# Four graph layers in one kernel: the end of the first output chunk of the second pass comes four products later

## The chip, the cores and the metric

The kernel runs on one core of a Trainium2 chip. The metric is the device time of one execution in microseconds (us). The time before is 1056.23 us, the median of three runs (1054.62 to 1058.79). The profile is one more execution, with a time of 1041.55 us.

## The reference

A graph of N = 2708 nodes has a sparse-looking but densely stored weight matrix `adj` (N x N, f32) and 128 features a node (`x`). Four layers follow one another, each as `x = layernorm(x + layer(x, adj))`. What matters here is layer 0 and the start of layer 1:

```python
# layer 0
z = leaky_relu(lap_mul(A, x) @ W1 + b1, 0.1)
S = exp(-sqrt(max(|z_i - z_j|^2, 0) + 1e-10) / 2), kept for the 4 nearest rows j of each i, else 0
out = lap_mul(S + A, x) @ W2 + b2          # lap_mul(A, x) = d * (A @ (d * x)), d = rowsum(A)^-1/2
# layer 1
XW = X @ W;  s_col = XW @ a[:128];  s_row = XW @ a[128:]
den = exp(leaky_relu(s_row[:, None] + s_col[None, :], 0.01))
num = A @ den;  att = den / num;  H = A @ (att @ XW)
# layer 2: normalized adj @ x, a linear map;  layer 3: relu of a linear map of [x, adj @ x]
```

The product `(S + A) @ (d * x)` of layer 0 is the second pass over `adj`: a dense part, `A` times the scaled rows, and a sparse part, four gathered rows for each node, weighted by their similarity. From the result layer 1 needs the rank of every node by `s_col`, which the kernel finds by comparing every pair.

## The kernel before

Nodes are cut into T = 22 tiles of 128 (the last has 20 rows), and the columns of the transposed output into six chunks: four of 512, one of 384 and one of 276. Chunk 0 holds tiles 0 to 3, chunk 1 tiles 4 to 7, and so on.

The second pass is `by_panels` (line 189). For each chunk c it multiplies 21 row tiles (and, for three chunks together, the short last tile) into one PSUM tile `acc`: the `product` at line 204 has the scaled rows `y2` (name `y` in the profile) as weights and a stretch of `adjT` as moving data. One product is two MATMUL entries in the trace. Row tiles 16 to 21 of `adjT` stay in SBUF (`res`), the others come from memory in panels of four row tiles (1 MB, line 178, issued on SP) into four slots of `ring`. A slot is filled again when the four products that read it are done.

Between the products everything else of the pass is put by hand. TensorE, VectorE (DVE) and ScalarE (ACT) run in exactly the order in which the program names their instructions (`manual_schedule`, line 1064). `Due` (line 31) is a list of work with due counts: `due.tick()` runs after each product, counts up by one, and issues all work that is due. I call this number the count. GpSimd (POOL) and SP are not under the manual order.

The work with due counts:

- `sum_near(t)` (line 765), at the counts 20 + (24 t) // 5, so 20, 24, 29, 34, 39, 44, 48, 53, 58 for tiles 0 to 8. On POOL three indirect DMAs (line 759) each gather 128 rows of 512 bytes from memory into one of nine `got` buffers; on DVE one TENSOR_SCALAR (line 768) and three SCALAR_TENSOR_TENSOR (line 772) add them up, each of the three behind its own gather.
- `end_pass2(c, acc)` (line 1014), called when chunk c has its last product. It puts the end of the chunk on a count n, and all that follows from it on n plus a fixed number:
  - n: `add_near` (line 774), which multiplies the chunk's `near_sum` tiles with the identity into `acc` on TensorE (line 779, two MATMUL entries a tile), and the copy of `acc` to `hT` on ACT (line 1021);
  - n + 2: `norm0`, the product with W2 (line 809), the residual on DVE (line 814), and the layer norm (lines 272 to 277);
  - n + 9: `turn`, the transposes of the normalized rows on TensorE (line 827) and their copy on ACT (line 830);
  - n + 11: `find_c`, one product (line 883), its copy (line 884) and four reductions on DVE (line 888);
  - n + 13 and later, every second count: `compare` on DVE (lines 924 and 934), `times_w` (line 896 on TensorE, 897 on ACT), `rank_rows` on ACT (line 942), `rank_columns` on TensorE (line 947), and `keep_xw`, a DMA from POOL (line 902).

The count n is the largest of three: the next count, the count of the chunk's last `sum_near` plus 3, and the last chunk's n plus 16. For the six chunks this gives 37, 56, 75, 95, 111 and 132. For chunk 0, whose products end at count 21, it is the second term: tile 3 is due at 34, so n = 37.

The order of row tiles in chunk 0 is 0 to 11, 16 to 19, 12 to 15, 20. In chunk 1 the four products of the panel with row tiles 12 to 15 are those of the counts 37 to 40.

Of the kernel before, what the change touches and what calls it, by code (L numbers as in the profile page):

```python
# [30 lines left out]
class Due:  # L31
# [5 lines left out]
    def at(self, n, f, *args):  # L37
        self.work.append((n, len(self.work), f, args))
        self.work.sort(key=lambda w: w[:2])
# [13 lines left out]
def kernel(  # L53
# [47 lines left out]
    chunk_tiles = [range(a // P, (a + w + P - 1) // P) for a, w in zip(starts, cw)]  # L101
# [262 lines left out]
    with tc.tile_pool(name="knn", bufs=1) as knn:  # L364
# [68 lines left out]
        due = Due()  # L433
# [340 lines left out]
    def add_near(c, acc):  # L774
        ts = chunk_tiles[c]
        for t in ts:
            p = pw[t]
            o = t * P - starts[c]
            nc.tensor.matmul(
                acc[:, o : o + p], lhsT=near_sum[:p, t, :], rhs=ident[:p, :p], start=False, stop=(t == ts[-1])  # L780
            )
# [214 lines left out]
    due = Due()  # L996
    at = due.at
    near_at = [20 + (24 * t) // 5 for t in range(T)]
# [11 lines left out]
    ended = [-16]  # L1010
# [1 line left out]
    behind_turn = []  # L1012

    def end_pass2(c, acc):
        n = max(due.n + 1, near_at[chunk_tiles[c][-1]] + 3, ended[-1] + 16)
        ended.append(n)
        ts = chunk_tiles[c]

        def finish():
            add_near(c, acc)  # L1020
            nc.scalar.copy(hT[:, cols[c]], acc[:, : cw[c]])

        at(n, finish)
        if c < C - 1:
            at(n + 2, norm0, ts)
            at(n + 9, turn, c)
            at(n + 11, find_c, c)
            if c == C - 2:
                for t in behind_turn:
                    at(n + 11, rank_rows, t)  # L1030
            for k, t in enumerate(ts):
                at(n + 13 + 2 * k, compare, t)
                at(n + 14 + 2 * k, times_w, c, t)
                if k == len(ts) - 1:
                    at(n + 14 + 2 * k, keep_xw, c)
                if c == C - 2 and k == len(ts) - 1:
                    behind_last.append(t)
                elif c == C - 3 and k == len(ts) - 1:
                    behind_turn.append(t)
                else:  # L1040
                    at(n + 16 + 2 * k, rank_rows, t)
                if t:
                    at(n + (20 if c < C - 2 else 18) + 2 * k, rank_columns, t)
        else:
            for t in behind_last:
                at(n + 1, rank_rows, t)
            at(n + 2, norm0, ts, True)
            at(n + 2, turn, c, True)
            at(n + 2, exp_table)
            at(n + 2, find_r)  # L1050
            at(n + 3, last_stats)
            at(n + 3, last_of, 1, cc)
            at(n + 3, turn_c, c)
            at(n + 3, compare_known, ts[0])
            at(n + 5, last_of, 0, rr)
            at(n + 5, negate_r)
            for k, t in enumerate(ts[:-1]):
                at(n + 4 + k, compare, t)
                at(n + 4 + k, rank_rows, t)
                at(n + 5 + k, rank_columns, t)  # L1060
            at(n + 3 + len(ts), compare_few)
            at(n + 4 + len(ts), exp_r)

    with tc.manual_schedule(engines={nc.tensor.engine, nc.vector.engine, nc.scalar.engine}):
        by_panels(
            rows_of(y2), end_pass2, due.tick, ready, [*range(S - 4), *range(S, T - 2), *range(S - 4, S), T - 2]
        )
        due.flush()
# [814 lines left out]
```

## Time and profile before

| what | value |
|---|---|
| median of three runs | 1056.23 us |
| the profiled execution: time, span | 1041.55 us, 1039.7 us |
| TensorE busy over the span | 973.5 us (94%) |
| DVE, ACT, POOL busy | 639.0, 332.2, 261.0 us |
| mean granted TensorE clock | 0.983 |
| second pass in the span | about 285 to 418 us |
| dense products in it (line 204), each of two entries | about 0.86 us each at 512 columns |

The profile's page gives shares over the whole span; all times inside the second pass below are microseconds from the span's start. In a timeline an entry has its start, its length and, in brackets, how long the engine stood idle before it and what ended that. "PE" is TensorE. In a table by windows each engine's busy time in that stretch is followed by the number of instructions in brackets, and the columns at the end are the granted TensorE clock (1.00 is full), the busy share of the DMA engines, and GB/s.

### The profile page before, as it was taken

The numbers are of one execution on the slowest core, as the hardware profiler recorded it, in microseconds if no ns is written. First come the engines' busy times: TensorE is split into PE (matmuls) and PEld (weight loads), VectorE is DVE, ScalarE is ACT, GpSimd is POOL, SyncE is SP. The second block draws the span as 40 slices with busy tenths as digits, with TensorE's granted clock in tenths as the row PEclk, the third lists the DMA queues.
The fourth block names the chain that finished last, engine by engine and source line by source line (L and its number), as shares of the span: only waits on it lengthen the run. The fifth ranks groups of instructions, "written<-read, shape, count | busy, mean of one in ns | idle before, by whom it ended". The sixth has DMA issues, their size and how long they took to land.

```text
span 1039.7 us, 11663 instructions
## 1 busy us (share of the span) xinstructions
PE 973.5 (94%) x3773; PEld 476.7 (46%) x3773; DVE 639.0 (61%) x1364; ACT 332.2 (32%) x609; POOL 261.0 (25%) x339
## 2 busy tenths in 40 slices
PE   0789999999998999797999999999999999999996
PEld 0346554444444557563333333334445544564444
DVE  5886438999955678865899999992212021222222
ACT  0000126555501236505777777661101100020000
POOL 4000000000557664027565444420111100000000
PEclk9999999999998999799999999999999999999999
DMA  9999240000175757696465455556565856475652
GB/s 328 373 365 314 91 152 1 0 1 1 43 240 183 236 171 239 236 409 204 144 163 158 131 144 160 143 178 238 165 229 151 310 181 224 137 273 173 212 179 68
DMA packets 101985, 191.00 MB, mean 184 GB/s; under 512 B 14006, under 2 KB 43326, under 8 KB 101914
## 3 DMA queue, kind: packets, MB, share of 16 engines
q1 hardware_dynamic: 83880, 152.34, 43.5%
q0 software_dynamic: 17728, 37.62, 12.6%
q8 instruction: 32, 0.52, 0.2%
q14 instruction: 39, 0.32, 0.1%
q10 hardware_dynamic: 306, 0.20, 0.1%
HBM read 214.80 MB, written 4.16 MB: 211 GB/s over the span
## 4 chain that ended last, share of the span: by engine, by line
PE 50%; DVE 1%; ACT 1%; issue 0%; DMA 0%; POOL 0%; POOLq 0%; DVEq 0%
PE acc L204 28%; PE hacc L1571 10%; PE num L1689 10%; PE mis L285 1%; PE mis L1818 0%; DVE inv L1560 0%; DMA ring<-carry 0%; ACT gb L234 0%; DVE err L1556 0%; PE mis L1784 0%; DVE inv L1563 0%; PE mis L1814 0%; POOL rstd L253 0%; PE mis L1772 0%; ACT m_rows L160 0%
## 5 line engine op out<-in xcount | busy, mean ns | idle before, releaser
L1689 PE MATMUL num<-ring,lw 128*64 128x512 f32 (+1 forms) x528 | 112.1, 557 | 5.4 <-DMA ring<-carry 2.9
L1123 POOL DMA_INDIRECT ring<-in_adjT,slot_i x88 | 92.9, 1056 | 96.6 <-PE num L1689 77.5
L1571 PE MATMUL hacc<-inv,xws 128*128 128x512 f32 (+1 forms) x264 | 111.7, 559 | 0.3 <-DVE inv L1563 0.3
L714 PE MATMUL acc<-zT,z 128*128 128x512 f32 (+2 forms) x252 | 102.2, 552 | 0.0
L1546 ACT ACTIVATE inv<-num,plain 128x1024 f32<-128x1024 f32 x88 | 80.6, 916 | 59.0 <-PE num L1689 43.1
L253 POOL TENSOR_TENSOR rstd<-rstd,minus_half 128x4 f32<-128x4 f32 (+1 forms) x18 | 17.3, 959 | 311.8 <-DVE rstd L252 311.8
L234 ACT COPY gb<-acc 128x512 f32<-128x512 f32 (+2 forms) x18 | 9.6, 534 | 249.4 <-PE acc L204 249.4
L715 ACT COPY key<-acc 128x512 f32<-128x512 f32 (+2 forms) x126 | 67.1, 534 | 55.1 <-PE acc L714 27.7
L204 PE MATMUL acc<-ring,y 128*128 128x512 f32 (+2 forms) x192 | 82.1, 557 | 0.5 <-issue 0.5
L1571 PEld LDWEIGHTS hacc<-inv,xws 128*128 128x128 f32 x264 | 46.6, 189 | 77.8 <-issue 33.5
L1556 DVE TENSOR_TENSOR err<-inv,num 128x1024 f32<-128x1024 f32 x88 | 74.7, 853 | 10.1 <-ACT inv L1549 8.9
L759 POOL DMA_INDIRECT got<-y_rows,where x66 | 71.4, 1081 | 34.6 <-DVE near_sum L772 13.5
L1563 DVE SCALAR_TENSOR_TENSOR inv<-gb,g_inv,inv 128x1024 f32<-128x1024 f32 x88 | 77.0, 913 | 0.1
L204 PE MATMUL acc<-ring,xs 128*128 128x512 f32 (+2 forms) x192 | 76.7, 542 | 0.0
L204 PE MATMUL acc<-ring,carry 128*128 128x512 f32 (+2 forms) x192 | 74.5, 542 | 0.0
L204 PE MATMUL acc<-ring,m_rows 128*128 128x512 f32 (+2 forms) x192 | 74.3, 542 | 0.0
L1560 DVE SCALAR_TENSOR_TENSOR inv<-err,inv 128x1024 f32<-128x1024 f32 x88 | 72.4, 861 | 0.1
L714 PEld LDWEIGHTS acc<-zT,z 128*128 128x128 f32 x252 | 45.8, 190 | 50.4 <-issue 44.9
L1549 ACT ACTIVATE inv<-inv 128x1024 f32<-128x1024 f32 x88 | 67.6, 768 | 2.8
L1689 PEld LDWEIGHTS num<-ring,lw 128*64 128x64 f32 x528 | 36.1, 137 | 62.9 <-issue 48.1
L584 POOL TENSOR_TENSOR slot_e<-near,sim 128x44 f32<-128x44 f32 (+2 forms) x3 | 0.7, 237 | 254.5 <-DVE near L581 254.4
L718 DVE MAX8 near<-key 128x8 f32<-128x2708 f32 x21 | 62.3, 2965 | 2.6 <-ACT key L715 2.6
(379 smaller groups left out, 1355.7 us busy)
## 6 DMA issues: line engine op xcount, KB each, us to landing
ring<-in_adjT SPq DMA_DIRECT2D x74, 1024.0 KB
ring<-in_adjT SPq DMA_DIRECT2D x20, 677.0 KB
ring<-in_adjT SPq DMA_DIRECT2D x17, 768.0 KB
part<-in_adjT SPq DMA_DIRECT2D x12, 1024.0 KB
ring<-in_adjT SPq DMA_DIRECT2D x17, 552.0 KB
more<-in_adjT SPq DMA_DIRECT2D x10, 677.0 KB
res<-in_adjT SPq DMA_DIRECT2D x4, 1280.0 KB
part<-in_adjT SPq DMA_DIRECT2D x3, 768.0 KB
```

The source lines that it names most:

```text
L204: nc.tensor.matmul(accs[c][: lhsT.shape[-1], :w], lhsT=lhsT, rhs=src, start=start, stop=stop)
L714: nc.tensor.matmul(pks[c][:p, : cw[c]], lhsT=z2[:, :p], rhs=zT[:, cs], start=False, stop=True)
L715: nc.scalar.copy(key[:p, cs], pks[c][:p, : cw[c]])
L759: nc.gpsimd.indirect_dma_start(out=got[:p, :], out_offset=None, in_=y2_rows[:, :], in_offset=bass.IndirectOffsetOnAxis(ap=where[:p, t, k : ...
L1123: nc.gpsimd.indirect_dma_start(out=rows[i][:KC, n, :], out_offset=None, in_=adj_half[:, :], in_offset=bass.IndirectOffsetOnAxis(ap=slot_i[ ...
L1546: nc.scalar.activation(inv, num[:, :w], AF.Ln, scale=plain[:, 0:1], bias=plain[:, 1:2])
L1549: nc.scalar.activation(inv, inv, AF.Exp, scale=-1.0)
L1556: nc.vector.tensor_mul(err, inv, num[:, :w])
L1560: nc.vector.scalar_tensor_tensor(inv, err, 2.0, inv, op0=ALU.subtract, op1=ALU.mult)
L1563: nc.vector.scalar_tensor_tensor(inv, gb[:, col : col + w], g_inv[:, q : q + 1], inv, op0=ALU.max, op1=ALU.mult)
L1571: nc.tensor.matmul(haccs[:, o:e], lhsT=xws[:, q, :], rhs=inv[:, o:e], start=(q == 0), stop=(q == NQ - 1))
L1689: nc.tensor.matmul(num[n * (BJ + 2) : (n + 1) * (BJ + 2), o:e], lhsT=lw[:, 2 * q + n, :], rhs=rows[i][:, n, c0 + o : c0 + e], start=True, ...
```

## The change

One number in `end_pass2` is replaced: chunk 0 now ends at least 7 counts after its last `sum_near`, the other chunks still at least 3.

```diff
     def end_pass2(c, acc):
-        n = max(due.n + 1, near_at[chunk_tiles[c][-1]] + 3, ended[-1] + 16)
+        n = max(due.n + 1, near_at[chunk_tiles[c][-1]] + (3 if c else 7), ended[-1] + 16)
         ended.append(n)
```

The counts n of the six chunks become 41, 57, 75, 95, 111 and 132. Chunk 0 moves by four; chunk 1 moves by one, because it has to stay 16 behind chunk 0; the others stay. No instruction is added or removed. The order of the instructions on POOL and SP stays as it was. On TensorE, DVE and ACT the work of chunks 0 and 1 changes places with its neighbours: on DVE `sum_near` of tile 7 now stands ahead of the first `compare` of chunk 0, the `compare` of tile 3 behind the layer norm of chunk 1, and `sum_near` of tile 10 ahead of the reductions of `find_c` for chunk 1; on ACT and TensorE the end of chunk 1 comes earlier among the row sums and the `times_w` of chunk 0.

## The prediction

> **What bounds the kernel now.** Over the span TensorE is busy 94%, so only its losses in the second pass count. I read first the second pass by windows: before the end of chunk 0, around it, the long middle, the end.
>
> ```profile
> core 0: us, PE busy (x) PEld busy (x) DVE busy (x) ACT busy (x) POOL busy (x), PEclk, DMA share, GB/s
> 285.00:314.45 29.45, 29.45 (x73) 12.65 (x72) 16.05 (x44) 2.43 (x11) 16.93 (x31) 1.00 0.73 243
> 314.45:325.00 10.55, 6.38 (x21) 4.11 (x20) 3.06 (x8) 1.87 (x2) 8.11 (x9) 0.68 0.52 173
> 325.00:415.00 90.00, 88.84 (x468) 52.99 (x468) 67.52 (x253) 33.71 (x72) 54.33 (x51) 1.00 0.65 205
> ```
>
> TensorE is full up to 314.45 and almost full after 325.00. Between, it is busy 6.38 of 10.55 us, and at a clock of 0.68. So the second view is TensorE's timeline there:
>
> ```profile
> 314.45 0.83 PE L779 MATMUL acc<-ident,near_sum 128*128 128x128 f32 x6
> 319.46 0.80 PE L779 MATMUL acc<-ident,near_sum 128*128 128x128 f32 x2 [4.17 <-DVE near_sum L772]
> 320.05 3.62 PE L204 MATMUL acc<-ring,y 128*128 128x512 f32 x4
> 323.46 1.80 PE L809 MATMUL mis<-w,hT 128*128 128x128 f32 x8
> 325.10 1.02 PE L204 MATMUL acc<-ring,y 128*128 128x512 f32 x2
> 325.96 4.46 PE L204 MATMUL acc<-res,y 128*128 128x512 f32 x10
> ```
>
> At 314.45 chunk 0 ends: three tiles of near rows go through (x6), the fourth stands 4.17 us for DVE. After it four entries of the dense product take 3.62 us; later ten take 4.46. The clock by windows, cut where it changes, says why (same columns):
>
> ```profile
> 314.77:318.18 3.41, 0.52 (x5) 0.32 (x3) 0.70 (x2) 0.00 (x0) 2.74 (x3) 1.00 0.93 309
> 318.18:321.60 3.42, 2.14 (x4) 1.27 (x5) 0.91 (x3) 1.29 (x2) 2.51 (x4) 0.50 0.39 126
> 321.60:325.00 3.40, 3.40 (x11) 2.21 (x10) 1.44 (x4) 0.58 (x1) 2.79 (x3) 0.50 0.20 59
> 325.00:328.40 3.40, 3.40 (x10) 1.62 (x10) 2.76 (x13) 0.14 (x1) 2.49 (x4) 1.00 0.40 90
> ```
>
> The nearly idle window is followed by 6.8 us at half clock. Last, DVE's timeline: what the fourth tile waits for.
>
> ```profile
> 315.79 0.74 DVE L772 SCALAR_TENSOR_TENSOR near_sum<-got,sim,near_sum 128x128 f32<-128x128 f32 x2 [1.96 <-DMA got<-y_rows,where]
> 319.06 0.35 DVE L772 SCALAR_TENSOR_TENSOR near_sum<-got,sim,near_sum 128x128 f32<-128x128 f32 x1 [2.53 <-DMA got<-y_rows,where]
> 319.32 0.43 DVE L768 TENSOR_SCALAR near_sum<-y,own_sim 128x128 f32<-128x128 f32 x1
> 321.39 1.13 DVE L772 SCALAR_TENSOR_TENSOR near_sum<-got,sim,near_sum 128x128 f32<-128x128 f32 x3 [1.63 <-DMA got<-y_rows,where]
> 322.43 0.68 DVE L1002 TENSOR_TENSOR xs<-xs,b 128x512 f32<-128x512 f32 x1
> 325.30 1.13 DVE L814 SCALAR_TENSOR_TENSOR xs<-mis,d2inv,xs 128x128 f32<-128x128 f32 x4 [2.19 <-PE mis L809]
> ```
>
> Its third gather has landed only at 319.06, and DVE is free before. The gathers start at 298.93 and POOL issues one every 1.30 us; none of the first twelve waits for a product. So tile 3 is ready at 319.41 whatever TensorE does: the end of chunk 0 comes too early for the gathers. This wait is the only one of TensorE in the pass over 1.3 us.
>
> [...] the gathers issued between 312 and 318, beside panel loads, take a median of 5.4 us to land, those between 322 and 330 take 2.5. [...]
>
> **The change part by part.** No instruction is added or removed, and POOL's and SP's orders stay.
>
> Part 1, the loss now. From 314.45 to 325.96 (11.51 us) TensorE does the near rows of four tiles, three dense products and eight entries of the W2 product. At full clock, from undisturbed places of this trace: 0.89 us (341.66 to 342.55), 3 x 0.858 (ten entries at 325.96 take 4.29 to the next start), 0.89 (344.49 to 345.38), together 4.35. The loss is 11.51 - 4.35 = 7.16 us: 4.3 of standing still (tile 3 due at 314.45 + 6 x 0.111 = 315.12, started at 319.46) and 2.8 of half clock.
>
> Part 2, what remains of it. Four products go ahead: the end of chunk 0 starts at 314.45 + 4 x 0.858 = 317.88, tile 3 is due at 318.55 and comes at 319.46 as before. Remaining wait 0.91 us. Does the clock hold? The trace bounds it: with 2.65 of 3.41 us busy (406.93:410.34) it stayed at 1.00, with 1.96 of 3.41 (417.17:420.58) it fell. A window with 0.9 us of idling is 2.5 busy, near the first. I take no throttle: half clock 0 (bound: one window, 1.7 us).
>
> Part 3, the DMA that moves along. In chunk 1 the last of the four products reading a ring slot is that of count 40. Before, it was over at 326.1, behind the stall, and SP issued the panel load at 326.15. Now it comes before the end of chunk 0, at about 317.0, and the 1 MB load goes out nine us earlier, right behind the one of 313.79. Tile 3's gathers are issued before that (the last at 313.53), so I leave 319.41. But the last gather of tile 4 is issued at 317.44, after the load. By the semaphore events of the trace these panel loads land 5.1 to 7.3 us after issue, so this one at 322.1 to 324.3, and with it that gather, instead of at about 321.7.
>
> Part 4, who waits for that. On DVE `sum_near` of tile 4 stands ahead of the bias (0.68 us) and the layer norm of chunk 0. If nothing slips, DVE is through the bias at 323.11; the W2 product, now at full clock, is at 319.68 + 2 x 0.858 = 321.4 to 322.3. So the norm starts at 323.1 instead of 325.3. It takes 4.5 us (325.30 to 329.83): done at 327.6. The transposes need it, seven products after W2: 322.3 + 7 x 0.858 = 328.3. Slack 0.7. With the gather landing at 322.1 to 324.3, the norm starts at about 323.3 to 326.1 (0.35 for the last addition, 0.68 the bias, some overlap of 0.1 each) and ends at 327.8 to 330.6: TensorE waits 0 to 2.3 us there. I take a landing of 323.1, so a wait of 0.7; both ends go into the range.
>
> Part 5, the rest of the moved chain keeps its cover. Copy to `hT` on ACT: 0.58 us under two products (1.72), as before. `find_c` to `compare` on DVE: same counts apart. `sum_near` of tile 7 now stands ahead of the compares: gathers issued up to 329.5, landed by 334 to 335, added by 336; chunk 1 ends at count 57, about 337 with part 4's wait, its fourth tile 0.7 later. If that cover were gone it would cost what the landing is late. `compare` of tile 3 and `times_w` of tile 3 move behind chunk 1's norm in DVE's and ACT's queues; the row DMA to memory that needs them stands in POOL's queue at 346.27 and needs them by about 344, so it isn't held. Chunk 1's one product more is not work, only order: 0.
>
> Part 6, does the lead survive? DVE stands 4.1, 4.2, 1.9 and 4.5 us for TensorE between 341 and 377 and POOL stands 3.9, 2.8, 1.3 and 3.1 us for freed buffers between 346 and 379, so both can follow 5 to 6 us earlier. From 377 to 415 DVE has under 1 us of gaps, but that stretch begins behind a TensorE product and moves with it. From chunk 2's norm on every order is the old one. After the pass the line loads start when TensorE has freed the ring, so they move too. I take all of it as kept.
>
> The sum: 7.16 - 0.91 - 0.7 = 5.5 us. Against the profiled execution: 1041.55 - 5.5 = 1036.0. The median of the runs is 14.7 us above that execution; I carry the same difference over: 1056.23 - 5.5 = 1050.7, or 0.52% less.
>
> **The rivals.**
>
> Rival 1, the clock falls again: tile 3 or the transposes wait more than about 1.4 us inside one window (1.96 of 3.41 busy was enough). For it: part 3's load lands late, 324.3, giving a wait of 2.3. Against: usual landings are nearer 5.2. Price: 1.6 more waiting and 1.7 for one window at half clock: gain 5.5 - 3.3 = 2.2; 1.5 to 4.5 with smaller slips. Time 1054.0.
>
> Rival 2, the lead is given back at the end of the pass: DVE is busy 8.9 of 10 us and ACT 9.7 of 10 in its last 20 us, and TensorE already waits there for masks (1.2 and 1.1 us). If they don't start earlier, gain 0 to 2: 1055.2. Against: part 6.
>
> Rival 3, slower: the held-back gather of tile 4 makes a larger stall at the transposes than the one removed. Place: DVE's queue, gather, bias, norm, then TensorE at count 50. Price: [...] the loss is 0.91 + s + 2.8 against 7.16. From s = 3.5, a landing at about 325.9, it is even; slower by 0.5% (5.3 us) needs s = 8.7, a landing at 331, over 13 us after issue, where the trace has at most some 6.5. Time then 1062.
>
> Rival 4, in the timed runs the old stall is longer than in the profiled one (they are longer altogether, and the profile doesn't say where): four products can absorb up to 3.43 us of wait, the half clock could be longer: gain 7 to 9, time 1048.
>
> That the change doesn't do what it says is excluded: the counts come out of the code as 41 and 57.
>
> **How the numbers follow.** Forecast (gain 4.8 to 6.3) 0.62; rival 1 0.20; rival 2 0.08; rival 3 0.04; rival 4 0.06. About 0.5% (5.3 us) is what a measurement of this kernel can tell from no change. It cuts through my forecast: of 0.62 I put 0.44 above it; with rival 4 faster 0.50. Within 0.5%: 0.18 of the forecast and rivals 1 and 2, 0.46. Slower: 0.04. The range: the forecast alone 1049.9 to 1051.4, with the scatter of a median of runs (the three lie 1.6 below and 2.6 above) 1048 to 1054; to rival 4 below and rival 1 above, it becomes 1046.5 to 1055.
>
> **What would show it.** Right: line 779's wait falls from 4.17 to about 0.9 us, the clock stays 1.00 between 314 and 330, a panel load is issued near 317 and not at 326, chunk 1 ends at count 57 at about 337 instead of 341.66. Part 4: a wait of up to 2.3 us at line 827 for DVE's norm. Wrong: a clock of 0.50 in that stretch, tile 3's last addition later than 320, or chunk 5's end less than 4 us earlier than 415.02.

## The result, and the profile after it

| | before | changed |
|---|---|---|
| median of 22 runs each | 1057.16 us | 1057.76 us |
| lowest to highest | 1051.42 to 1061.24 | 1048.95 to 1063.06 |
| ratio, 95% interval | | 1.0015 [0.9997, 1.0033] |
| profiled execution: time, span, clock | 1041.55, 1039.7, 0.983 | 1057.04, 1055.2, 0.976 |

The change makes no difference that can be measured. I had forecast 1050.7 us, and the result lies outside my range.

A sitting is one series of runs, with the kernel before run again in it. The kernel before took 1040.2 to 1042.5 us in two of the seven sittings (this result is one of the seven) and 1056.7 to 1060.6 in the other five; two chips showed both. I call these short and long sittings. The profile shown ahead of the prediction is one of the short kind; the runs beside it, and the profile after, are of the long kind.

The second pass of the changed kernel by windows, cut where the end of chunk 0 begins, where the loss is over, and at the last chunk's near rows (columns as before):

```profile
285.00:317.91 32.91, 32.91 (x82) 14.17 (x80) 18.39 (x50) 2.44 (x11) 20.48 (x35) 1.00 0.70 233
317.91:339.00 21.09, 9.32 (x28) 5.29 (x27) 4.90 (x20) 2.08 (x3) 8.43 (x9) 0.68 0.37 127
339.00:425.98 86.98, 83.74 (x453) 50.13 (x452) 64.36 (x236) 33.35 (x71) 50.06 (x46) 1.00 0.62 197
```

The first window is full, up to 317.91 and no longer to 314.45: the four products have gone ahead. But then TensorE is busy 9.32 of 21.09 us, where before it was 6.38 of 10.55. Its timeline there:

```profile
317.91 1.05 PE L779 MATMUL acc<-ident,near_sum 128*128 128x128 f32 x8
318.80 1.88 PE L204 MATMUL acc<-res,y 128*128 128x512 f32 x4
332.45 2.08 PE L809 MATMUL mis<-w,hT 128*128 128x128 f32 x8 [11.77 <-ACT hT L1021]
334.32 3.62 PE L204 MATMUL acc<-res,y 128*128 128x512 f32 x4
337.74 4.79 PE L204 MATMUL acc<-ring,y 128*128 128x512 f32 x10
```

The wait of the prediction is gone: all eight entries of line 779 go through in one group. In its place the product with W2 (line 809), two products later, waits 11.77 us for ACT's copy of `acc` to `hT`. The clock by windows:

```profile
320.70:324.70 4.00, 0.00 (x0) 0.00 (x0) 0.95 (x2) 0.00 (x0) 3.08 (x4) 1.00 0.24 73
324.70:328.10 3.40, 0.00 (x0) 0.00 (x0) 0.00 (x0) 0.00 (x0) 2.49 (x4) 0.51 0.14 39
328.10:331.50 3.40, 0.00 (x0) 0.00 (x0) 0.00 (x0) 0.00 (x0) 0.68 (x1) 0.50 0.13 39
```

TensorE, DVE and ACT do next to nothing together; only POOL works. The clock is halved from 324.7 for 13.7 us. In the profiles before and after the stretches of half clock last 3.41, 6.83 or 13.65 us, save the last one of each (6.88 and 8.98 us). Why does the copy start so late? ACT's timeline has it at

```profile
331.81 0.59 ACT L1021 COPY hT<-acc 128x512 f32<-128x512 f32 x1 [36.09 <-remote]
```

although the matmuls that it needs were over at 318.96. ACT was free for 36 us, and "remote" means that the profile finds no event on this core that released it. The trace has the missing piece in the times at which TensorE's completions were counted in its semaphore (from here on "count" means this, not the due count of `Due`): those of the matmuls that ended about 317 to 319 were all counted between 330.89 and 331.79, in one burst, up to 13.7 us late. In the profile before, each such count comes within 0.3 us. SP's panel loads, which wait for the same semaphore, are held alike: line 178 issues one at 316.20 and the next only at 330.91. POOL's timeline shows what ends in between:

```profile
326.47 1.00 POOL L759 DMA_INDIRECT got<-y_rows,where  x1 [0.30 <-issue]
327.78 1.00 POOL L759 DMA_INDIRECT got<-y_rows,where  x1 [0.30 <-issue]
339.95 1.00 POOL L759 DMA_INDIRECT got<-y_rows,where  x1 [11.17 <-DVE near_sum L772]
```

From 297.64 on POOL has issued 24 gathers without a break. At 328.78 its nine buffers are all taken, it stops, and 3.0 us later the copy starts. DVE is not late with the near rows but stands, too:

```profile
317.10 0.74 DVE L772 SCALAR_TENSOR_TENSOR near_sum<-got,sim,near_sum 128x128 f32<-128x128 f32 x2
321.68 0.35 DVE L772 SCALAR_TENSOR_TENSOR near_sum<-got,sim,near_sum 128x128 f32<-128x128 f32 x1 [3.84 <-DMA got<-y_rows,where]
321.95 0.68 DVE L1002 TENSOR_TENSOR xs<-xs,b 128x512 f32<-128x512 f32 x1
334.57 1.13 DVE L814 SCALAR_TENSOR_TENSOR xs<-mis,d2inv,xs 128x128 f32<-128x128 f32 x4 [11.93 <-PE mis L809]
```

Tile 3's rows are added by 316.8, tile 4's last at 322.0. So the question is: is the late counting a thing of the changed order, or was it in the timed runs of the kernel before as well?

### The profile page after: what moved, and what is told of

Its sections match the earlier page's. It is cut to its first block, busy times and chain, and to the rows that moved or that the text cites. A ratio compares the mean times of both kernels' runs of the same rounds, so it can differ in the third digit from the quotient of the medians.

```text
span 1055.2 us, 11662 instructions
## 1 busy us (share of the span) xinstructions
PE 980.4 (93%) x3773; PEld 478.9 (45%) x3773; DVE 640.1 (61%) x1364; ACT 332.4 (32%) x609; POOL 261.8 (25%) x339
## 4 chain that ended last, share of the span: by engine, by line
PE 49%; DVE 1%; ACT 1%; issue 0%; DMA 0%; POOL 0%; POOLq 0%; DVEq 0%
PE acc L204 28%; PE hacc L1571 10%; PE num L1689 9%; PE mis L285 1%; PE mis L1818 0%; DVE inv L1560 0%; DMA ring<-carry 0%; ACT gb L234 0%; DVE err L1556 0%; PE mis L1784 0%; DVE inv L1563 0%; PE mis L1814 0%; POOL rstd L253 0%; PE mis L1772 0%; ACT m_rows L160 0%
## 5 line engine op out<-in xcount | busy, mean ns | idle before, releaser
L204 PE MATMUL acc<-ring,y 128*128 128x512 f32 (+2 forms) x192 | 79.6, 548 | 0.5 <-issue 0.5
```

Source lines behind the costliest of these rows:

```text
L204: nc.tensor.matmul(accs[c][: lhsT.shape[-1], :w], lhsT=lhsT, rhs=src, start=start, stop=stop)
```

## The experiments

Where the expectations name theories by letters, A says that late counts come in both kernels and depend on the sitting; B that the changed order brings them about; C that they are held while POOL issues gathers without a break, so that the stall ends when POOL runs out of buffers; D that panel loads or chance hold them. All times after a colon are medians; every ratio is to the kernel before in the same sitting.

### Both kernels again, chunk 0 without gathers, and seven made eleven

e1 is the kernel before unchanged, e2 the changed one. e3 is the kernel before without the gathers and additions of tiles 0 to 3 (their near rows are left out of the sum). e4 takes the change further.

```diff
 # e3
-        for k in range(TOPK - 1):
+        for k in range(TOPK - 1 if t > 3 else 0):
 # e4
-... near_at[chunk_tiles[c][-1]] + 3, ended[-1] + 16)
+... near_at[chunk_tiles[c][-1]] + (3 if c else 11), ended[-1] + 16)
```

> The kernel before, unchanged, with a second profile. Theory A: the late semaphore counts of TensorE (13.7 us late in the profile after, ACT and TensorE idle for 11.8 us) come in ordinary executions of either kernel, and the first profile of before, at 1041.55 us, was an exceptional one: this profile shows a span near 1052 to 1056 with a stall of about 10 us in the second pass that is not the wait for near_sum alone. Theory B: the late counts come with the changed order only: this profile shows a span near 1040, one stall of 4 us at line 779 and no other over 2 us in the second pass. Time ratio 1.00 in both.

> The changed kernel, unchanged, with a second profile. Theory A: in some profiles a stall of about 10 us at the first copy of acc or the W2 product, in others none and then a span of about 1036. Theory B: the stall of 11.8 us at the same instruction again. Time ratio 1.00 in both.

> The kernel before with the gathered rows of tiles 0 to 3 left out (near_sum there is only the node's own row), so that the end of chunk 0 at count 37 waits for no gather. If the wait for near_sum and its half clock are what costs (my prediction's part 1): 7.2 us less than before, ratio 0.993. Theory A: another stall takes its place in most executions and the ratio lies between 0.997 and 1.002. Theory B: 7.2 us less.

> Chunk 0 ends at count 45 (11 after its last near_sum), chunk 1 at 61, chunk 2 at 77. By the prediction's reasons: the wait at line 779 is gone altogether and tile 4's gather has time, 6 to 7 us less than before (ratio 0.994). Theory A: ratio 0.998 to 1.003 as the change of four had, with the stall at whatever waits first for TensorE's count. Theory B: the stall of 12 us at the copy of acc again, ratio about 1.00.

Measured, with the kernel before at 1042.54 us (33 runs), so in a short sitting: e1 1043.16, ratio 1.0008 [0.9993, 1.0022]; e2 1038.26, **0.9951 [0.9930, 0.9972]**; e3 1039.76, 0.9978 [0.9968, 0.9989]; e4 1036.91, 0.9937 [0.9916, 0.9957]. The long stall came in none of the four, so what these expectations say of it stays unanswered here. In time the changed kernel (five runs) gains what the prediction said, e4 (five runs) what its expectation said; e3 misses its 0.993. TensorE's timeline in e2:

```profile
318.20 0.83 PE L779 MATMUL acc<-ident,near_sum 128*128 128x128 f32 x6
320.11 0.49 PE L779 MATMUL acc<-ident,near_sum 128*128 128x128 f32 x2 [1.07 <-DVE near_sum L772]
320.43 1.88 PE L204 MATMUL acc<-res,y 128*128 128x512 f32 x4
322.15 1.05 PE L809 MATMUL mis<-w,hT 128*128 128x128 f32 x8
323.04 1.88 PE L204 MATMUL acc<-res,y 128*128 128x512 f32 x4
324.76 4.45 PE L204 MATMUL acc<-ring,y 128*128 128x512 f32 x10
330.08 1.10 PE L827 MATMUL mis<-ident,xs 128*128 128x128 f32 x4 [0.87 <-DVE xs L277]
```

A wait of 1.07 us for tile 3 where I had 0.91, one of 0.87 at the transposes where I had 0.7, no half clock in this stretch, a panel load at 317.54 where I had about 317. DVE's line for the last near row of tile 4:

```profile
325.40 0.35 DVE L772 SCALAR_TENSOR_TENSOR near_sum<-got,sim,near_sum 128x128 f32<-128x128 f32 x1 [4.36 <-DMA got<-y_rows,where]
```

The pass shows the lead, and how more than half of it is lost: counted from the pass's first product, the end of chunk 1 comes at 54.1 us (e1: 56.8), though it stands one product of 0.86 us later in the changed order, so the lead there is 3.6 us of work; the end of chunk 5 comes at 128.5 (e1: 130.1), a lead of 1.6. These two executions are not typical: e1's is the shortest of its twelve (1039.01 us), e2's the longest of its five (1040.88). So the traces don't show where the whole gain of the medians lies. e3 gains more inside the pass (chunk 5 at 123.9) and less in all: its trace has the clock halved for 13.1 us at the very end, where e1 has 9.4, and once more at 937.9.

### The kernel before in a long sitting

f1 is the kernel before, unchanged, profiled where it is slow.

> The kernel before, unchanged, once more, in the hope of a chip on which it takes 1057 us as in the comparison of the result, not 1042 as in the last runs. Theory A (the late semaphore counts belong to such a chip, whatever the kernel): if the time is near 1057, the profile shows a stall of some 10 us behind a late count in the second pass, fewer semaphore events recorded than in the first profile, and a granted clock near 0.976. Theory B (they belong to the changed order): no such stall, and the 15 us are spread or lie elsewhere. If the time is near 1042 it tells nothing new.

Measured: 1061.08 against 1060.52, ratio 1.0006 [0.9993, 1.0018]. TensorE's timeline of f1:

```profile
313.92 0.83 PE L779 MATMUL acc<-ident,near_sum 128*128 128x128 f32 x6
316.82 0.49 PE L779 MATMUL acc<-ident,near_sum 128*128 128x128 f32 x2 [2.06 <-issue]
317.14 3.29 PE L204 MATMUL acc<-ring,y 128*128 128x512 f32 x4
333.39 2.08 PE L809 MATMUL mis<-w,hT 128*128 128x128 f32 x8 [12.96 <-ACT hT L1021]
```

The same stall, in the same place, in the kernel before: B falls, A stands. The wait for tile 3, from which my whole sum was made, is 2.06 us here and is followed by 12.96 us for the copy. POOL again issues 24 gathers, the last over at 329.70, and the copy starts at 332.75, 3.05 us later. This one execution took 1066.16 us, the most of its twelve and 5.1 above their median. With that taken off, as if all of it lay in the pass, chunk 5 ends 144.2 us after the pass's start (149.3 in the trace) by my estimate, in the changed kernel at 142.0 (its execution 0.7 below its median) and in g1, below, at 140.5 (5.6 below). The two kernels' passes are alike.

### Chunk 0 without gathers, and fewer buffers, in a long sitting

g1 is the changed kernel, g2 is e3's kernel again, with the same near rows left out; g3 and g4 are the kernel before and the changed one with five buffers for gathers in place of nine, so that POOL has to stop earlier.

```diff
-    got_pool = late.enter_context(tc.tile_pool(name="got", bufs=9, side="right"))
+    got_pool = late.enter_context(tc.tile_pool(name="got", bufs=5, side="right"))
```

> The changed kernel again. Two conditions have been seen: before at 1042 us (there the change gave a ratio of 0.995) and before at 1057 to 1061 (there 1.0015). Theory C: in the slow condition TensorE's counts are held back as long as POOL issues gathers without a pause, so the copy of acc to hT comes when POOL has run out of got buffers (about 331 to 333), wherever the end of chunk 0 stands: ratio 0.995 to 1.003, stall of 11 to 13 us in front of the W2 product. Theory D: the held-back count is a matter of the panel loads or of chance, not of POOL. In the fast condition: 0.995 again.

> The kernel before without the gathered rows of tiles 0 to 3 (left out). POOL then has 12 gathers less and runs out of buffers at about 314, before the end of chunk 0. Slow condition, theory C: no stall at the copy of acc, 12 to 20 us less than before (ratio 0.981 to 0.989). Theory D: the stall stays, at most 4 us less. Fast condition: 0.998 as before.

> The kernel before with five got buffers instead of nine: POOL must stop four gathers earlier, at about 325 instead of 330, as DVE has then used the gathers of tiles 0 to 4 only. Slow condition, theory C: the stall ends about 5 us earlier, 4 to 8 us less than before (ratio 0.992 to 0.996). Theory D: same as before or slower. Fast condition: 0 to 3 us slower, since gathers start later.

> The changed kernel with five got buffers. Slow condition, theory C: the stall in front of the W2 product ends about 5 us earlier than with nine, ratio 0.990 to 0.996 against before. Theory D: as the changed kernel. Fast condition: 0.994 to 0.999.

Measured, kernel before at 1056.69 (63 runs): g1 1057.58, 1.0007 [0.9986, 1.0027]; g2 1052.97, 0.9967 [0.9947, 0.9987]; g3 1057.03, 1.0003 [0.9984, 1.0022]; g4 1057.54, 1.0017 [0.9997, 1.0038]. g1 repeats the result. The gains expected of g2 to g4 did not come, or came too small. In g4 POOL pauses after 14 gathers, at 316.64, and stops after 20, at 325.69. The copy starts at 321.30, between the two and 1.7 us after its matmuls, and the first stall is gone: TensorE waits nowhere in the pass more than 2.3 us, and chunk 1 ends 55.3 us into it (66.2 in the profile after). Yet chunk 5 ends at 139.4: TensorE stands 10.9 us in all, in short waits (5.4 in e1); what makes up the rest is open. In g2 the stall at line 809 comes with chunk 1 instead (3.81 us, at 338.8), and that copy starts 1.6 us after POOL's last gather; in g3 the first copy starts at 328.35, while POOL is issuing again after a pause.

g1 speaks against C as it was put. Its last gather before the stop, and its copy:

```profile
329.48 1.00 POOL L759 DMA_INDIRECT got<-y_rows,where  x1 [0.30 <-issue]
330.65 0.59 ACT L1021 COPY hT<-acc 128x512 f32<-128x512 f32 x1 [34.37 <-issue]
```

The copy starts 0.2 us after POOL's stop, and five counts of TensorE came one by one before it, at 317.79, 320.77, 323.58, 326.40 and 328.51, while POOL was issuing. f1 has two such, at 320.79 and 326.37. Records may be missing between them. So the counts come slowly while the gathers go out, rather than being held until the last is out; and moving POOL's stop did not win the time.

### Plain DMAs, no gathers at all, and eleven, in a long sitting

h1 replaces each gather by a plain DMA from POOL of the same size, which loads the node's own rows (other data are added). h2 leaves out all gathers and their additions. h3 is e4 again.

```diff
 # h1
-        nc.gpsimd.indirect_dma_start(out=got[:p, :], ... in_=y2_rows[:, :], in_offset=...)
+        nc.gpsimd.dma_start(got[:p, :], y2_rows[t * P : t * P + p, :])
 # h2
-        for k in range(TOPK - 1):
+        for k in range(0):
```

> The kernel before, with every gather of sum_near replaced by a plain DMA from POOL of the same size (128 rows of 512 bytes, the node's own rows, so the near rows that are added are other data). Same number of DMAs, bytes and additions. Theory 'held counts' (TensorE's completion counts come late while POOL issues indirect DMAs): where the kernel before is at about 1057 on this chip, no stall of over 6 us at line 809 or 779 in the second pass, chunk 5's end about 130 us after the pass's start instead of 140 to 149, ratio 0.975 to 0.992; where the kernel before is at about 1042, only the wait for tile 3 goes, ratio 0.993 to 0.998. Rival 'any POOL DMA or the DMA traffic itself holds the counts': at 1057 the ratio stays 0.997 to 1.003 and a stall of 6 us or more is in the pass.

> The kernel before without any gather or addition of near rows in the second pass (the sparse part is only each node's own row). It is the floor of what the gathers cost: where the kernel before is at about 1057, the theory of held counts says 0.975 to 0.990 and a second pass at the pace of the quick runs (chunk 5's end some 126 to 130 us after the pass's start); at about 1042, 0.992 to 0.998. If the plain DMAs of the run beside it stand nearer to this run than to the kernel before, it is the indirect form that costs. If this run, too, is within 0.5% of the kernel before at 1057, the slow pass has nothing to do with POOL's gathers.

> The change taken further: chunk 0 ends at least 11 counts after its last sum_near (counts 45, 61, 77, 95, 111, 132). It was 0.9937 with the kernel before at 1042.5. At about 1042 I expect 0.992 to 0.996 again. At about 1057 the theory that POOL's gathers and TensorE's chain of the chunk's end cannot overlap says that due counts do not matter: 0.998 to 1.002 as with seven; the rival, that TensorE only needs enough products that wait for no late count, says 0.990 to 0.996.

Measured, kernel before at 1060.40 (27 runs): h1 1041.29, **0.9813 [0.9790, 0.9835]**; h2 1037.81, 0.9777 [0.9755, 0.9799]; h3 1063.83, 1.0036 [1.0020, 1.0053]. h1 is the clearest of all runs: as many DMAs, bytes and additions, on the same DMA queue (2560 packets before and 2528 in h1 from 284 to 424 us), and 19.1 us less. Of the 22.6 us that the gathers and their additions cost in this sitting (h2) all but 3.5 go with the indirect form. More than the form is changed by that: a plain DMA takes POOL 0.58 us on average (a gather 1.08), the first nine leave from 282 us on and not from 299, and they read rows that lie one behind the other. h1 does not separate these. The panel loads are in h1 as before, so they alone (D) are not enough.

h1 and h2 have four runs each. That they ran in the long condition, and not by chance in the short one, can be seen in their own traces. Behind the pass POOL issues other indirect DMAs (lines 1099 and 1119 of h1). There some of TensorE's counts come up to 1.5 us late, and from 433 to 700 us the trace holds only 2824 (h1) and 2655 (h2) semaphore events, like f1 (2795) and unlike e1 (3818) of a short sitting. In the pass itself, where these two kernels issue no indirect DMA, no count is over 0.3 us late. In the short sittings' traces none is in either stretch.

h1's TensorE timeline has not one wait where the stalls were (line 775 is the former 779, 805 the former 809):

```profile
314.36 1.05 PE L775 MATMUL acc<-ident,near_sum 128*128 128x128 f32 x8
315.25 1.88 PE L204 MATMUL acc<-ring,y 128*128 128x512 f32 x4
316.97 1.05 PE L805 MATMUL mis<-w,hT 128*128 128x128 f32 x8
```

Chunk 5 ends 123.9 us after the pass's start, where the profiles of the short sittings with all gathers have 127 to 131 and those of the long ones 139 to 149. h3, which as e4 was the best of the short sitting, is the worst here, a little above what either theory expected. Its trace says how: TensorE

```profile
323.42 1.05 PE L779 MATMUL acc<-ident,near_sum 128*128 128x128 f32 x8
324.31 1.88 PE L204 MATMUL acc<-ring,y 128*128 128x512 f32 x4
338.78 2.08 PE L809 MATMUL mis<-w,hT 128*128 128x128 f32 x8 [12.59 <-ACT hT L1021]
```

and POOL:

```profile
333.50 1.00 POOL L759 DMA_INDIRECT got<-y_rows,where  x1 [0.30 <-issue]
346.27 1.00 POOL L759 DMA_INDIRECT got<-y_rows,where  x1 [11.78 <-DVE near_sum L772]
```

With eleven, `sum_near` of tile 5 stands ahead of chunk 0's norm in DVE's queue and frees three more buffers; POOL issues 27 gathers instead of 24, stops at 334.50, and the copy comes 3.6 us after that. So in three traces (the profile after, f1 and h3) the copy follows POOL's stop by 3.0 to 3.6 us, wherever the chunk's end was put; in g1 it was 0.2.

### A rest between gathers, and the change with plain DMAs

i1 and i2 put a rest of POOL ahead of each tile's gathers into the kernel before and the changed one, i3 a longer one ahead of tiles 3 to 14 of the changed one. i4 is h1 with the change.

```diff
 # i1, i2, and with 12 columns if 3 <= t < 15 i3; `rest` is a buffer that nobody reads
+        nc.gpsimd.tensor_tensor(rest, ones8, minus_half[:, :6], op=ALU.pow)
         for k in range(TOPK - 1):
```

> The kernel before, and ahead of each tile's three gathers POOL raises six columns to a power into a buffer that nobody reads (about 1.3 us by the row of line 253, so the gathers come in threes with a rest instead of one train). If the unbroken train holds TensorE's counts, no stall is longer than about 6 us, and with the kernel before at 1057 to 1060 the ratio is 0.985 to 0.997 (tile 3's rows come 4 us later, so its wait at line 779 grows). If the number of indirect DMAs counts, 0.999 to 1.006. Where the kernel before is at 1042: 1.001 to 1.006, the rows only come later.

> The changed kernel with the same rest ahead of each tile's gathers. If the train holds the counts: 0.980 to 0.992 with the kernel before at 1057 to 1060, and 3 to 6 us below the run with the rest but without the change, since tile 3's rows come late and the four products cover that. If not: 0.999 to 1.006, as the change alone.

> The changed kernel with a rest of about 2.3 us (twelve columns) ahead of the gathers of tiles 3 to 14 only. If the train holds the counts: like the run before it, 0.980 to 0.993 with the kernel before at 1057 to 1060. If not: 0.999 to 1.006.

> The changed kernel with plain DMAs of the node's own rows in place of the gathers (so other near rows are added), to be set beside the kernel before with the same plain DMAs, which took 0.9813 of the kernel before at 1060.4. There nothing waited at line 779 and no count came late, so four products more ahead of the chunk's end should be worth nothing: 0.979 to 0.984 at 1057 to 1060. If the change has a price or a gain of its own besides the near rows, it shows here: below 0.977 or above 0.986.

Measured, kernel before at 1040.17 (23 runs), a short sitting: i1 1061.09, 1.0210 [1.0168, 1.0253]; i2 1061.90, 1.0213 [1.0170, 1.0256]; i3 1059.25, 1.0195 [1.0151, 1.0238]; i4 1036.24, 0.9958 [0.9942, 0.9973]. The first three are a flaw of mine, and POOL's timeline of i1 shows it:

```profile
336.87 1.00 POOL L762 DMA_INDIRECT got<-y_rows,where  x1 [0.30 <-DVE own L892]
337.90 19.90 POOL L772 TENSOR_TENSOR rest<-ones,minus_half 128x6 f32<-128x6 f32 x14
357.97 1.06 POOL L762 DMA_INDIRECT got<-y_rows,where  x1 [0.17 <-issue]
```

POOL's order is not kept by hand. The rests wait for nothing, so fourteen of them stood in one block, and the gathers of tile 8 came 20 us late. These runs say nothing of the theory; they do show that gathers 20 us late go with 20.9 us more (i1).

i4 answers its question from the traces, one execution of each kernel. With plain DMAs chunk 5 ends at 123.9 us into the pass with the change and, in h1, at 123.9 without: four products more ahead of the chunk's end are worth nothing when no near row and no count is late. My number for i4 was made for a long sitting and can't be held against it. The two kernels' times (1036.24, 1041.29) are of different sittings; h1's trace has the clock halved for 6.8 us at 485, after the pass, where i4's has none.

### The rest in its place

In j1 (kernel before) and j2 (changed kernel) the rest is written into the first gather's own buffer, which the gather then overwrites, so it stands directly ahead of it.

```diff
+            if k == 0:
+                nc.gpsimd.tensor_tensor(got[:p, :6], ones8[:p], minus_half[:p, :6], op=ALU.pow)
             gather_near(got, t, TOPK + k)
```

> The kernel before; ahead of each tile's three gathers POOL writes six columns of the first gather's own buffer (1.4 us by the rows of the runs before), which the gather then overwrites, so the rest stands where it is put. Tile 3's rows come about 5 us later, so the wait at line 779 becomes 9 us where it was 4.2, and later chunks may wait for rows too. Where the kernel before takes about 1040: 1.004 to 1.012. Where it takes 1057 to 1060, and the unbroken train holds TensorE's counts: 0.985 to 0.998; if the number of gathers counts and not their train: 1.003 to 1.010.

> The changed kernel with the same rest in the same place. The four products more cover 3.4 us of tile 3's later rows, so it should be 0.003 to 0.008 below the run beside it, in ratio, at either time of the kernel before, if the train holds the counts; if the counts come late all the same at 1057 to 1060, equal to it within 0.003 there.

Measured, kernel before at 1060.58 (43 runs): j1 1062.48, 1.0021 [1.0007, 1.0035]; j2 1062.07, 1.0011 [0.9996, 1.0025]. In time both miss what C expected: j1 lies nearer to what was expected if the number of gathers counts (1.003 to 1.010), and j2 is within 0.003 of j1, as was expected if counts come late all the same. What TensorE waits for in the pass has changed, though. The table of waits (total, number, longest) of f1, without rests:

```profile
PE mis L809 <- ACT hT L1021: 15.9, 3, 13.0
PE mis L883 <- ACT xT L830: 2.3, 2, 1.5
PE acc L779 <- issue: 2.1, 1, 2.1
```

and of j1 (783 is the former 779, 831 the former 827):

```profile
PE acc L783 <- DVE near_sum L776: 9.2, 3, 3.7
PE mis L831 <- DVE xs L277: 1.9, 1, 1.9
PE rk L951 <- DVE mask L928: 1.3, 1, 1.3
```

No long wait for a copy is left; the waits are for near rows, which come late because the rests take 1.4 us a tile. Chunks 1 to 3 end at 59.1, 79.8 and 100.4 us, nearly the pace of the short sittings (56.8, 77.5, 97.1; f1 69.8, 94.9, 114.5), and chunk 5 at 146.1, as late as ever. In j1's pass no count of TensorE is over 0.3 us late up to 380 us; some records are missing there all the same. That fits the part of C that says that gathers without a break delay the counts, but it doesn't prove it: no time is won, since in the pass TensorE waits 9.2 us for near rows and has 23.9 us of half clock (13.7 in the profile after), and each is one execution.

## Why the prediction was wrong

- **Part 1, the loss.** Right for the profile. In e1, of a short sitting, the wait is 4.24 us, but the clock is halved for 3.4 us only, so the loss is 6.2 by the same working. In the long ones the loss at this place is another: 12.96 us of waiting at line 809 for counts, with 13.7 us of half clock (f1), and only 2.06 us at line 779.
- **Part 2, the wait for tile 3.** Right where the kernel was as profiled: 1.07 us for 0.91, and a clock of 1.00 from 314.45 to 331.00 (e2). What idling halves the clock was my estimate, here and in rival 1, from two stretches of one trace; no run measured it.
- **Part 4, the wait at the transposes.** 0.87 us for 0.7 in e2, but in part by luck. Its sum doesn't come out of its own terms: 0.35 and 0.68 less two overlaps of 0.1 put the norm 0.83 us behind the landing, which gives 325.1 and not 326.1 for a landing at 324.3, and almost no wait for one at 323.1. In e2 the last row of tile 4 came at 325.4, 7.4 us after its issue, later than part 4's range and more than the "some 6.5" of rival 3 (where s is the stall at the transposes, and the half clock that it brings an estimate). The norm began 0.87 us after it, and the transposes began at 330.08, before the norm's last step was over at 330.79, where I had let them wait for all of it. Two errors offset each other.
- **Part 3, the panel load.** It left at 317.54 in e2, as worked out. In the profile after it left at 330.91, when its count came (330.89). That tile 4's last gather would land with it was my estimate. In the profile before, the load of 313.79 had its last semaphore event at 321.09 and the gathers issued behind it, at 314.83, 316.14 and 317.44, had theirs at 321.29, 321.49 and 321.65; why they land so close to it was not shown.
- **Part 5, the cover of the copy to `hT`.** "0.58 us under two products (1.72), as before." This is the cover that was gone in the long sittings, in both kernels: the copy is as short as ever (0.59), but its start hangs on a count that came 13 us late.
- **Part 6, the lead.** In e2's profile 3.6 us of work at chunk 1's end and 1.6 at chunk 5's, so 2 us were given back inside the pass, not nothing; a part of rival 2 is true. One of the prediction's own signs of being wrong came even here: chunk 5's end at 412.75 is less than 4 us earlier than 415.02.
- **The sum.** 5.5 us; in the short sitting the ratio 0.9951 is 5.1 us [2.9, 7.3] of 1042.5. The size holds there, on five runs, and the waits of parts 1 and 2 behave as said; where in the kernel the whole gain lies is not shown.
- **The step that failed** is the last one: "The median of the runs is 14.7 us above that execution; I carry the same difference over". That difference is no constant that the change leaves alone. Most of it lies in this very pass (e1 130.1, profile after 142.0, f1 149.3 us to chunk 5's end; between e1 and f1 19.2 of the 27.2 us by which the executions differ), begins at the very place that the change moves, and takes away the loss that I had counted: there the copy waits for a late count until 331.8 us with the change and 332.8 without (f1), wherever chunk 0 ends. Rival 4 was the warning ("the profile doesn't say where"), but it only allowed for more gain; I should have allowed that the stall of the timed runs is of another kind.

What is settled: the long stall is in both kernels (f1); it goes when plain DMAs take the gathers' place (h1); and the gathers alone don't make it, for in the short sittings POOL issues the same unbroken train of gathers (from 298.93 past 343.97 in the profile before) and no count is late; with rows and counts in time the change is worth nothing inside the pass (i4 beside h1). What stays open: why the counts come late, whether it takes the indirect form itself or the long train that it makes, what a long sitting is, and why g4, which lost the first stall, won nothing in all. One hint: where counts are late the trace also holds fewer records. From 284 to 424 us it holds 2151 semaphore events before, 2232 in h1, but 989 after, 940 in f1. Whether recording has a part in the late counts was not shown; no run was made without it.

## What to carry to other kernels

When the profiled execution lies outside the scatter of the timed runs by more than the gain that is to be forecast, find out first where the difference lies; a sum made inside such a profile may count a loss that the timed runs don't have. A wait that ends "remote" (in g1 "issue") with everything of this core long done was a late count here: look at what the others that wait for the same semaphore do, here SP's panel loads. Of two versions measured in one sitting the better one may be the worse in another, as eleven was (0.9937 and 1.0036), so repeat both kernels together in more than one.

## What the runs showed of the hardware

- In the long sittings TensorE's completions were counted late while POOL issued indirect DMAs every 1.30 us: up to 13.7 us and in a burst in the profile after, one by one and 2.1 to 3.0 us apart in g1. The waiting copy started 3.0, 3.05 and 3.6 us after POOL's last one (profile after, f1, h3), and 0.2 us after it in g1.
- Sixty-six indirect DMAs of up to 128 rows of 512 bytes cost 19.1 us more than plain ones of the same size in a long sitting (h1). With all gathers gone in the kernel before the gain was 22.6 us (h2).
- The same kernel took 1042.5 us in one sitting and 1060.5 in the next on one chip, 1040.2 and 1060.6 on another.
- Six columns raised to a power on POOL took 1.36 us (i1), twelve 2.31 us (i3).
